# v's 1x1 convolution inside the scan of the image before, two of v's taps as diagonal matmuls, and smaller moves of work between engines

## The chip, the cores and the metric

One NeuronCore of a Trainium2 chip runs the whole program. The time is the device time of one execution in microseconds; lower is better. Before the change, three runs gave 19038.22, 19043.21 and 19052.77 us, median 19043.21 us. Engines: PE is TensorE's matmul, PEld its weight load, DVE VectorE, ACT ScalarE, POOL GpSimd, SP SyncE, which here issues nearly all DMAs.

## What is computed

Eight images of 384 channels x 64 x 64, float32, one after the other. Each passes two layers with a residual.

```python
x = x + attention(groupnorm(x))        # layer 0
x = x + selective_scan(groupnorm(x))   # layer 1

# layer 0: 1x1 convolution, then a depthwise 3x3, for each of q, k, v
q = dwconv3x3(conv1x1(x, wq), dwq)     # the same for k and v
attn = softmax(l2norm(q) @ l2norm(k).T * temperature)   # 48x48 for each of 8 heads
out  = conv1x1(attn @ v, wproj)

# layer 1: 4 directions k, state size 16, 384 channels d, 4096 positions l
dts, Bs, Cs = split(x_proj[k] @ xs[k])
dt = softplus(dt_proj[k] @ dts + bias)
h[l] = h[l-1] * exp(dt * A) + (dt * u) * B[l]     # for every (d, n)
y[l] = sum_n h[l] * C[l]
# the four directions are added, a layer norm over channels and a gelu follow
```

## The kernel before

**Layout.** 384 channels are three blocks of 128 partitions (m or j = 0, 1, 2); 4096 positions are eight chunks of 512 (c). The loop over images b calls `channel_attention` and then `selective_scan`; the last layer norm and gelu of image b ("finishing") run inside the attention of image b+1, and after the last image in `finish`.

**Attention** works on 36 pieces of 16 image rows: 12 for k, 12 for q, then 12 for v (index t = 24 to 35, by row band p, then block m). A loop over t works on several pieces at a time: `bands` and `band` do the 1x1 convolution of piece t+2 (three matmuls for 8 rows, then ACT writes them with the bias, L370 and L374); `start_sum` and `end_sum` for piece t+1 form three tap products on ACT (L419), two sums of them on POOL (L426, L432), and put the product of the centre tap into a PSUM tile `ac`; `finish_sum` for piece t adds five taps to `ac` on DVE (L457) and the POOL sum (L462). Once the softmax is known (t = 27), `fold` makes one matrix of attention and projection; `project_in` then makes a 128x512 piece of the output by three matmuls (L603), and `project_out` adds it to x on DVE (L610), takes its statistics (L611) and stores it. The last six of these 24 come after the loop, mixed with the steps of `norm_factors` for the next image. `load_ahead` loads the next image's x in pieces for its statistics (L663).

**Scan.** 32 steps for each image: 4 directions times 8 chunks (s). One step is 12 units (r = 0 to 11: block j times group g of 4 states). A unit has four scans on DVE (L962, 512 positions each). Their inputs are `da`, an exponential on ACT (L938) in a PSUM ring of three, and `db` = w times B, one POOL product of 2048 elements (L950) in a ring of three. Four transposes on PE (L983), a copy out of PSUM on ACT (`hc`, L989) and four matmuls against `cp` (L1000) turn each state tile into y. Order on each engine is that of the program text (`pin`).

Once in a step, for the next one: `project` (24 matmuls of 128 columns over r = 0 to 5, into the one bank of pool `ps_m`), `lay_out` at r = 6 (copy to `xd` on ACT, stores to DRAM, loads `cx`), `mingle_c` at r = 7 (reorders C on POOL, L872), `turn_c` at r = 8 (one transpose into the `ps_m` bank), and at r = 9 what the text calls the burst: ACT changes to Softplus, makes three `dt`, and changes back to Exp, while DVE does two `take` and four products `cp` (L889). `weigh` makes w = x times dt on POOL (L921). `fetch` broadcasts B from DRAM by DMA.

Between attention and the first scan of an image lie the last norm, `project` and `lay_out` of step 0, three `dt`, three w on DVE, the first B by DMA and `drive(0)` on DVE (L950). ACT normalises nine pieces of x there (L1063). During step 3 `look_ahead` scales the next image's wk on ACT (r = 5) and makes its bias at r = 7: nine small matmuls on PE (L272) and one operation on DVE (L277).

Of the kernel before, what the change touches and what calls it, by code (L numbers as in the profile page):

```python
# [95 lines left out]
def tile_channel_attention_then_selective_scan(ctx: ExitStack, tc: tile.TileContext, a: dict):  # L96
# [183 lines left out]
    def load_wk(b):  # L280
        wk = big.tile([P, NJ, C], F32, tag="near", name=f"wk{b}")
        nc.sync.dma_start(wk, a["wk"].rearrange("(j p) o -> p j o", p=P))
        return wk
# [15 lines left out]
    def channel_attention(b, x, stats, before):  # L299

        pin = tc.keep_in_program_order
        with ExitStack() as st:
# [6 lines left out]
            mean, rstd, wk, bias_k = stats  # L309
# [13 lines left out]

            def load_w(n):
                wts[n] = wp.tile([P, NJ, C], F32, tag="wt", bufs=2, name=f"{n}{b}")
                nc.sync.dma_start(wts[n], a[n].rearrange("(j p) o -> p j o", p=P))
# [52 lines left out]
            def bands(t):  # L379

                w, m, p = pieces[t]
                y0 = PR * p
                if w == "v":
                    if p > 0 and m == 0:
                        if ("v", p) not in pres:
                            pres["v", p] = work.tile([P, L], F32, tag="pre", name=f"pre{b}v{p}")
                        lo = max(0, PR * (p - 1) - 1)
                        rows_ = (PR + 2) * W
                        old = pres["v", p - 1][:, : NJ * rows_].rearrange("p (m l) -> p m l", l=rows_)
                        new = pres["v", p][:, : NJ * rows_].rearrange("p (m l) -> p m l", l=rows_)  # L390
                        edges.append((new[:, :, : 2 * W], old[:, :, (y0 - 1 - lo) * W : (y0 + 1 - lo) * W]))
                    if p == 0:
                        return [(t, 0, BR), (t, BR, BR), (t, PR, 1)]
                    return [(t, y0 + 1, BR), (t, y0 + 1 + BR, BR - (p == NP - 1))]
                flat = range(2 * t + (t > 0), min(2 * t + 3, 2 * KQ))
                return [(n // 2, n % NCH * BR, BR) for n in flat]

            edges = []

            def rows_of(t):  # L400

                w, m, p = pieces[t]
                if w == "v":
                    rows_ = (PR + 2) * W
                    pre = pres[w, p][:, m * rows_ : (m + 1) * rows_]
                    return pre.rearrange("p (h w) -> p h w", w=W), max(0, PR * p - 1)
                return pres[w, m].rearrange("p (h w) -> p h w", w=W), 0
# [5 lines left out]
            def product(t, tap, dy, out=None):  # L413

                pre, lo = rows_of(t)
                y0 = PR * pieces[t][2] + dy - lo
                if out is None:
                    out = work.tile([P, PR, W], F32, tag="pr", bufs=4, name=f"pr{b}_{t}_{tap}")
                pin(nc.scalar.activation(out, pre[:, y0 : y0 + PR, :], AF.Copy, scale=weight(t, tap)))  # L419
                return out  # L420

            def start_sum(t):

                up = pieces[t][2] > 0
                q, left = product(t, 1 if up else 7, -1 if up else 1), product(t, 3, 0)
                pin(nc.gpsimd.tensor_add(q[:, :, 1:], q[:, :, 1:], left[:, :, : W - 1]))  # L426
                sums[t] = q

            def end_sum(t):
# [4 lines left out]
                product(t, 4, 0, accs[t])  # L434
# [11 lines left out]
            def finish_sum(t, mid):  # L446
# [4 lines left out]
                for tap in (0, 2, 6, 8, 7 if y0 else 1):  # L451
# [145 lines left out]
            pps = {}  # L597

            def project_in(m, c, js=range(NJ)):
                if (m, c) not in pps:  # L600
                    pps[m, c] = bank(f"pp{b}{m}_{c}")
                for j in js:
# [65 lines left out]
            for t in range(-2, T):  # L668
# [10 lines left out]
                elif t == 2:  # L679
                    load_w("wv")  # L680
                elif t == KQ - 7:
                    scale_w("v")
                elif t == KQ - 5:
# [17 lines left out]
                def half(h):  # L701
# [10 lines left out]
                    if t > KQ + 2:  # L712
                        next(last, None)
                        project()
                        next(last, None)

# [33 lines left out]
                while ready:  # L750
                    project_out(*ready.pop(0))
                if t > KQ + 2:
# [27 lines left out]
    def selective_scan(b, x1, stats1, after):  # L780

        y_d = dram.tile([L, C], F32, tag="yd", bufs=2, name=f"yd{b}")
        with ExitStack() as st:
# [18 lines left out]
            with tc.tile_pool(name=f"sn{b}", bufs=1, reuse_waits="tile") as np_:  # L802
# [5 lines left out]
                for c in range(5):  # L808
                    for j in range(NJ):
# [6 lines left out]
                        else:  # L816
# [3 lines left out]
                            ))  # L820
            def view(t, k, c):
# [47 lines left out]
            def mingle_c(s):  # L869

                cy = work.tile([NG * NQ, HP, NV], F32, tag="cy", bufs=1, name=f"cy{b}_{s}")
                pin(nc.gpsimd.tensor_copy(cy, cxs[s].rearrange("r v l -> r l v")))  # L872
# [11 lines left out]
            def spread_c(s, g):  # L884

                t = work.tile([P, NQ, HP], F32, tag="cp", bufs=8, name=f"cp{b}_{s}_{g}")
                c = pcts[s][:, g * NQ : (g + 1) * NQ].rearrange("p (q o) -> p q o", o=1)
                m = quad.rearrange("p (o l) -> p o l", o=1)
                pin(nc.vector.tensor_mul(t, m.broadcast_to([P, NQ, HP]), c.broadcast_to([P, NQ, HP])))  # L889
                cps[s, g] = t  # L890
# [25 lines left out]
            def weigh(s, j):  # L916

                k, c = steps[s][:2]
                eng = nc.vector if s == 0 else nc.gpsimd
                ws[s, j] = work.tile([P, CH], F32, tag="w", bufs=3, name=f"w{b}_{s}_{j}")  # L920
# [22 lines left out]
            def drive(u):  # L943
# [7 lines left out]
                dbs[u] = t  # L951

# [33 lines left out]
            def keep(u, lb):  # L986

                t = work.tile([P, NF, P], F32, tag="hc", bufs=6, name=f"hc{b}_{u}_{lb}")
# [3 lines left out]
            def add_up(u, lb):  # L992
# [5 lines left out]
                for f in range(NF):  # L998
                    q = NF * lb + f
                    pin(nc.tensor.matmul(  # L1000
                        py[f * HP : (f + 1) * HP, lb, :], lhsT=cps[s, g][:, q, :], rhs=hc[:, f, :],
# [28 lines left out]
            def sum_of(s, j):  # L1030

                sums[s, j] = work.tile([P, NLB, P], F32, tag="ysum", bufs=3, name=f"ys{b}_{s}_{j}")
# [15 lines left out]
            for j in range(NJ):  # L1048
                step_size(0, j, step_matmul(0, j))
                weigh(0, j)  # L1050
            warm = wp.tile([P, 1], F32, name=f"warm{b}")
            for g in range(1, NG):
                fetch(0, g)
            mingle_c(0)
            turn_c(0)
            drive(0)
# [3 lines left out]
            for c in range(5, NCH):  # L1060
                for j in range(NJ):
                    s = x1[j][:, bass.ts(c, CH)]
                    pin(nc.scalar.activation(  # L1063
                        s, s, AF.Identity, bias=shift[:, j : j + 1], scale=rstd[:, j : j + 1]
                    ))

            x_next, near = None, {}

            def look_ahead(u):
# [3 lines left out]
                if u == 2 * UN:  # L1073
                    near["w"] = load_wk(b + 1)
                if u == 3 * UN + 5:
                    scale_weights(near["w"], after[1])
                if u == 3 * UN + 7:
                    near["b"] = shift_of(big, ps_m, "m", near["w"], after[0], f"{b + 1}k")

            def unit(u):  # L1080
# [24 lines left out]
                if r in (2, 6, 10) and not last:  # L1105
                    sum_of(s, r // 4)
# [9 lines left out]
                if r == 7 and nxt:  # L1116
                    mingle_c(s + 1)
                if r == 10 and nxt:
                    weigh(s + 1, 0)
                if 0 < s < S and r in (0, 2):  # L1120
# [4 lines left out]
                added(2, o - 1)  # L1125
                decay(i0 + 2)
                kept(3, o - 1)
                if r == 6 and nxt:
# [9 lines left out]
                if burst:  # L1138
# [13 lines left out]
                    for g in range(NG):  # L1152
                        spread_c(s + 1, g)
# [5 lines left out]
                    kept(2)  # L1159
                    return  # L1160
# [10 lines left out]
                if nxt and r < 6:  # L1171
                    project(s + 1, 2 * r + 1)
                scanned(3)
                decay(i0 + 5)
                kept(2)

            for u in range(U + 1):
                look_ahead(u)
                unit(u)
                if u == 0:  # L1180
                    for g in range(NG):
                        spread_c(0, g)
# [6 lines left out]
            if x_next:  # L1189
                x_next = x_next, (*after, near["w"], near["b"])  # L1190
# [57 lines left out]
    with tc.tile_pool(name="pm", bufs=1, space=PSUM) as ps:  # L1248
# [3 lines left out]
        wk = load_wk(0)  # L1252
        scale_weights(wk, st0[1])
        x = x, (*st0, wk, shift_of(big, ps, "m", wk, st0[0], "0k"))
# [55 lines left out]
```

## Time and profile before

The profiled execution took 19037.42 us; its span is 19035.6 us. The spans of stages below are from the trace of the second image unless another is named; those of the others differ by a few microseconds.

| What | Time |
|---|---|
| last scan of an image to the first of the next | 415 to 423 us |
| first scan of an image to its last | 1943 to 1952 us |
| one step, directions 0 and 2 (median) | 60.67 us |
| one step, directions 1 and 3 (median) | 60.91 and 60.87 us |
| step 0 | 64.0 to 64.7 us |
| step 3, images 0 to 6 | 64.8 to 65.6 us |
| step 3, image 7 | 60.67 us |
| one scan on DVE, recorded, and from start to start | 1.27 and 1.18 us |
| `da` on ACT (L938) | 0.70 us |
| `hc` on ACT (L989) | 0.59 us |
| `db` on POOL (L950) | 4.59 us |
| five taps of one piece (L457), from start to start each | 1.31 us |

Recorded durations of neighbouring instructions overlap, so a sum of work is made from start to start: on ACT `da` and `hc` together take 1.09 us that way, and on PE a float32 product of 128x512 is two records of 0.43 us each.

### The profile page before, as it was taken

Reading aid. Unit: us, or ns where it says so; the run is one execution under the profiler, and the core shown is the slowest. Engines: PE = TensorE matmul, PEld = TensorE weight load, DVE = VectorE, ACT = ScalarE, POOL = GpSimd, SP = SyncE. Lnnn points to the kernel's source line nnn. Section 1 sums busy time; section 2 is a strip of 40 time slices with the busy share of each in tenths; the row PEclk is TensorE's granted clock in tenths of the full one; section 3 lists DMA queues with packets and bytes.
Section 4 is the critical chain, followed back from the end, with each engine's and each line's share of the span. In section 5 each row is a group of like instructions: output and inputs, shape, how many; then the busy total and the mean of one; then the engine's idle time right before and its main releaser. Section 6 shows DMA issues by size and latency. Waiting matters only on the chain. (4 is left out here: it accounts for less than half of the span.)

```text
span 19035.6 us, 415284 instructions
## 1 busy us (share of the span) xinstructions
PE 17213.2 (90%) x166560; PEld 9804.2 (52%) x166560; DVE 18353.2 (96%) x17552; ACT 17725.0 (93%) x29821; POOL 16891.1 (89%) x7491
## 2 busy tenths in 40 slices
PE   7999989999899998999989999899998999989998
PEld 4555545555455554555545555455554555545554
DVE  8999989999899998999989999899998999989999
ACT  6999979999799997999979999799997999979998
POOL 4999959999599995999959999599995999959998
PEclk9999999999999999999999999999999999999999
DMA  1233332333323333233332333223333233322333
GB/s 58 87 100 100 103 99 86 99 100 103 102 83 100 99 104 105 83 96 100 109 99 89 94 97 107 99 90 98 96 104 100 89 100 100 98 88 88 100 99 118
DMA packets 1199753, 1842.96 MB, mean 97 GB/s; under 512 B 154400, under 2 KB 1014816, under 8 KB 1060608
## 3 DMA queue, kind: packets, MB, share of 16 engines
q1 hardware_dynamic: 1196960, 1816.28, 29.8%
q8 instruction: 1314, 21.53, 0.5%
q14 instruction: 615, 5.04, 0.1%
q10 hardware_dynamic: 864, 0.12, 0.0%
HBM read 1497.29 MB, written 318.77 MB: 95 GB/s over the span
## 5 line engine op out<-in xcount | busy, mean ns | idle before, releaser
L950 POOL TENSOR_TENSOR db<-w,B 128x2048 f32<-128x2048 f32 x3072 | 14077.5, 4588 | 47.8 <-DVE h L962 24.9
L962 DVE TENSOR_TENSOR_SCAN h<-da,ca,db 128x512 f32<-128x512 f32 x10752 | 12723.9, 1265 | 30.7 <-ACT da L938 16.8
L983 PE MATMUL pt<-ident,h 128*128 128x128 f32 x49152 | 8164.9, 291 | 1079.4 <-ACT hc L989 882.1
L938 ACT ACTIVATE da<-dt,neg_a 128x512 f32<-128x512 f32 x12288 | 8616.7, 703 | 178.4 <-DVE h L962 171.3
L989 ACT COPY hc<-pt 128x512 f32<-128x512 f32 x12288 | 7265.4, 594 | 161.7 <-PE pt L983 77.0
L983 PEld LDWEIGHTS pt<-ident,h 128*128 128x128 f32 x49152 | 5324.2, 143 | 3958.9 <-ACT hc L989 2658.4
L1000 PE MATMUL py<-hc,cp 128*32 128x128 f32 x98304 | 5221.7, 289 | 1.2 <-ACT hc L989 1.2
L1000 PEld LDWEIGHTS py<-hc,cp 128*32 128x32 f32 x98304 | 1983.3, 109 | 2164.0 <-issue 2143.9
L962 DVE TENSOR_TENSOR_SCAN h<-da,db 128x512 f32<-128x512 f32 x1536 | 1739.5, 1209 | 65.1 <-ACT da L938 43.5
L426 POOL TENSOR_TENSOR pr<-pr,pr 128x1008 f32<-128x1008 f32 x288 | 673.1, 2337 | 1187.9 <-ACT pr L419 1156.8
L847 PE MATMUL px<-x,wx 128*44 128x128 f32 x6144 | 1580.2, 346 | 79.5 <-DVE cp L889 65.6
L921 POOL TENSOR_TENSOR w<-x,dt 128x512 f32<-128x512 f32 x744 | 1063.6, 1430 | 1.4 <-ACT dt L912 1.4
L847 PEld LDWEIGHTS px<-x,wx 128*44 128x44 f32 x6144 | 505.3, 120 | 663.5 <-issue 630.7
L904 PE MATMUL pd<-xd,wdt 128*128 128x512 f32 x1536 | 725.8, 608 | 97.5 <-DVE h L962 91.6
L432 POOL TENSOR_TENSOR pr<-pr,pr 128x1008 f32<-128x1008 f32 x288 | 574.9, 1996 | 230.7 <-ACT pr L419 165.2
L603 PE MATMUL pp<-v,mT 128*128 128x512 f32 x1152 | 545.7, 622 | 100.0 <-DVE v L462 98.9
L889 DVE TENSOR_TENSOR cp<-quad,pct 128x512 f32<-128x512 f32 x1024 | 630.4, 684 | 0.0
L976 POOL COPY ca<-h 128x4 f32<-128x4 f32 x2688 | 552.7, 206 | 0.0
L904 PEld LDWEIGHTS pd<-xd,wdt 128*128 128x128 f32 x1536 | 270.9, 189 | 397.4 <-issue 177.2
L912 ACT ACTIVATE dt<-pd,dt_bias 128x512 f32<-128x512 f32 x768 | 469.5, 679 | 2.1 <-PE pd L904 1.4
L1042 DVE TENSOR_TENSOR ys<-ys,py 128x512 f32<-128x512 f32 x576 | 388.5, 674 | 38.6 <-PE py L1000 38.6
L603 PEld LDWEIGHTS pp<-v,mT 128*128 128x128 f32 x1152 | 219.2, 198 | 359.3 <-issue 232.5
(337 smaller groups left out, 11426.5 us busy)
## 6 DMA issues: line engine op xcount, KB each, us to landing
B<-bcd SPq DMA_DIRECT2D x1024, 1024.0 KB, 5.1
yd<-ys SPq DMA_DIRECT2D x384, 256.0 KB, 5.3
ys<-yd SPq DMA_DIRECT2D x768, 128.0 KB, 3.0
yd<-ys SPq DMA_DIRECT2D x768, 128.0 KB, 5.2
x<-in_x SPq DMA_DIRECT2D x48, 1024.0 KB, 8.0
x1d<-x SPq DMA_DIRECT2D x192, 256.0 KB, 3.0
ys<-yd SPq DMA_DIRECT2D x192, 256.0 KB, 2.9
fy<-yd SPq DMA_DIRECT2D x128, 384.0 KB, 4.2
```

The costliest lines, as they stand in the source:

```text
L426: pin(nc.gpsimd.tensor_add(q[:, :, 1:], q[:, :, 1:], left[:, :, : W - 1]))
L603: pin(nc.tensor.matmul(pps[m, c], lhsT=fold_of[0][:, j, bass.ts(m, P)], rhs=vs["v"][:, j, bass.ts(c, CH)], start=j == 0, stop=j == NJ - 1,))
L847: pin(nc.tensor.matmul(split(pxs[s][:XR, :])[:, part, :], lhsT=wx[:, j, k, :], rhs=view(x1[j], k, c)[:, part, :], start=i == 0, stop=i == ...
L889: pin(nc.vector.tensor_mul(t, m.broadcast_to([P, NQ, HP]), c.broadcast_to([P, NQ, HP])))
L904: pin(nc.tensor.matmul(pd, lhsT=wdt[:, k, bass.ts(j, P)], rhs=xds[s], start=True, stop=True))
L921: pin(eng.tensor_mul(split(ws[s, j]), view(x1[j], k, c), split(dts[s, j])))
L938: pin(nc.scalar.activation(t, dts[s, j], AF.Exp, scale=neg_a[:, j, steps[s][0], n : n + 1]))
L950: pin(eng.tensor_mul(t, w.broadcast_to([P, NV, CH]), bts[s, g]))
L962: pin(nc.vector.tensor_tensor_scan(h, da, db, 0.0 if start else carries[s - 1][:, j, n : n + 1], ALU.mult, ALU.add,))
L983: pin(nc.tensor.transpose(t[:, f, :], hs[u][:, bass.ts(q, HP), :].rearrange("p l v -> p (l v)"), ident))
L989: pin(nc.scalar.copy(t, pts.pop((u, lb))))
L1000: pin(nc.tensor.matmul(py[f * HP : (f + 1) * HP, lb, :], lhsT=cps[s, g][:, q, :], rhs=hc[:, f, :], start=g == lb == 0, stop=g == NG - 1 an ...
```

## The change

It has six parts.

1. While image b is scanned, v's 1x1 convolution of image b+1 is made, for b = 0 to 6. Steps 3 to 26 each make one 128x512 piece: x of image b+1 is loaded every third step (r = 2), three matmuls stand at r = 9 (end of the burst), 10 and 11 in the `ps_m` bank, ACT writes the piece with its bias at r = 0 of the next step, and a DMA stores it to `v1_d`. wv is loaded at step 0 and scaled in steps 0 to 2 at r = 8, its bias made at step 3, r = 7; wk now comes in steps 28 to 31 in the same way. In the attention of image b+1 `load_v` reads v's bands from `v1_d` by four DMAs.
2. For those images, `add_by_pe` makes the centre tap and one more tap of v's pieces by matmuls with diagonal matrices (nine, made by DVE at the start of the attention), so ACT makes no centre product and `finish_sum` adds four taps on DVE.
3. At t = 35 the first two of three matmuls of four of the last six projections are issued.
4. At an image's start the first `db` is made from four matmuls that broadcast rows of `xd` (`first_drive`), third w goes to POOL at r = 2, and the nine normalisations of x are spread over steps 0 to 2. The Softplus table is asked for earlier.
5. `cp` is one DVE product of 2048 elements in place of four of 512.
6. `mingle_c` is a copy on ACT, at the end of r = 7, in place of POOL.

Ring sizes change too (`hc` 6 to 4, `w` 3 to 2, sums of y 3 to 2), and the loads of y move from r = 2, 6, 10 to r = 6, 7, 10.

```diff
+            if v1_d:
+                diag = wp.tile([P, NJ, 3, P], F32, name=f"diag{b}")
+                for m in range(NJ):
+                    for k in range(3):
+                        pin(nc.vector.tensor_scalar_mul(
+                            diag[:, m, k, :], ident, dws["v"][:, m, 3 * k + 1 : 3 * k + 2]
+                        ))
...
+            def load_v(p):
+                pres["v", p] = t = work.tile([P, L], F32, tag="pre", name=f"pre{b}v{p}")
+                r0, r1 = max(0, PR * p - 1), min(H, PR * (p + 1) + 1)
+                nc.sync.dma_start(
...
+            def add_by_pe(t):
+                pre, lo = rows_of(t)
+                m, y0 = pieces[t][1], PR * pieces[t][2] - lo
+                tap, dy, r0, r1 = far_tap(t)
+                for s, e in ((0, r0), (r0, BR), (BR, r1), (r1, PR)):
+                    both = r0 <= s and e <= r1
+                    for d, k in ((0, 4), (dy, tap))[: 1 + both] if e > s else ():
+                        pin(nc.tensor.matmul(
+                            accs[t][:, s:e, :], lhsT=diag[:, m, k // 3, :],
+                            rhs=pre[:, y0 + d + s : y0 + d + e, :], start=d == 0, stop=d != 0 or not both,
+                        ))
...
-                product(t, 4, 0, accs[t])
+                if helped(t):
+                    add_by_pe(t)
+                else:
+                    product(t, 4, 0, accs[t])
...
-                for tap in (0, 2, 6, 8, 7 if y0 else 1):
+                for tap in (0, 2, 6, 8) + (() if helped(t) else (far_tap(t)[0],)):
...
+                    if t == T - 1:
+                        for i in range(2 * h, 2 * h + 2):
+                            project_in(i % NJ, NCH - 2 + i // NJ, range(NJ - 1))
...
+                if v1_d and 0 <= cc < T:
+                    w, m, p = pieces[cc]
+                    if w == "q" and m > 0 and p == NP - 1:
+                        load_v(m - 1)
+                    elif w == "v" and m == NJ - 1 and p + 2 < NP:
+                        load_v(p + 2)
...
+            pin(nc.scalar.activation(warm, small["dt_bias"][:, 0, 0:1], AF.Softplus))
...
-                pin(nc.gpsimd.tensor_copy(cy, cxs[s].rearrange("r v l -> r l v")))
+                pin(nc.scalar.copy(cy, cxs[s].rearrange("r v l -> r l v")))
...
+                t = work.tile([P, n, HP], F32, tag="cp", name=f"cp{b}_{s}")
...
+            def first_drive():
+                t = dbs[0] = work.tile([P, NV, CH], F32, tag="db", bufs=3, name=f"db{b}_0")
+                for v, (pool, tag) in enumerate(((ps_y, "py"), (ps_y, "py"), (ps_m, "m"), (ps_t, "t"))):
+                    pb = pool.tile([P, CH], F32, tag=tag, name=f"pb{b}_{v}")
+                    pin(nc.tensor.matmul(
+                        pb, lhsT=ident[:, R + v : R + v + 1].broadcast_to([P, P]), rhs=xds[0],
+                        start=True, stop=True,
+                    ))
+                    pin(nc.vector.tensor_mul(t[:, v, :], ws[0, 0], pb))
...
+            first_drive()
             mingle_c(0)
             turn_c(0)
-            drive(0)
             drive(1)
...
+            def v_product(s, j):
+                if next_piece(s):
+                    c, m = next_piece(s)
+                    if j == 0:
+                        near["p"] = ps_m.tile([P, CH], F32, tag="m", name=f"pv{b}_{c}_{m}")
+                    pin(nc.tensor.matmul(
+                        near["p"], lhsT=near["v"][:, j, bass.ts(m, P)], rhs=near["x"][:, j, :],
+                        start=j == 0, stop=j == NJ - 1,
+                    ))
+            def v_store(s):
+                if next_piece(s):
+                    c, m = next_piece(s)
+                    t = work.tile([P, CH], F32, tag="va", bufs=1, name=f"va{b}_{c}_{m}")
+                    pin(nc.scalar.activation(t, near["p"], AF.Identity, bias=near["bv"][:, m : m + 1]))
+                    nc.sync.dma_start(v1_d[m, :, bass.ts(c, CH)], t)
...
-                if u == 3 * UN + 5:
-                    scale_weights(near["w"], after[1])
-                if u == 3 * UN + 7:
-                    near["b"] = shift_of(big, ps_m, "m", near["w"], after[0], f"{b + 1}k")
+                for n, w, s0 in (("v", "wv", 0), ("w", "wk", 28)):
+                    j = s - s0
...
+                    if 0 <= j < NJ and r == 8:
+                        pin(nc.scalar.activation(
+                            near[n][:, j, :], near[n][:, j, :], AF.Copy, scale=rstd[:, j : j + 1]
+                        ))
+                    if j == NJ and r == 7:
+                        near["b" + n] = shift_of(big, ps_m, "m", near[n], mean, f"{b + 1}{w[1]}")
...
+                if r == 2:
+                    v_load(s)
...
+                if r == 0:
+                    v_store(s - 1)
...
+                    v_product(s, 0)
                     return
...
+                if r > 9:
+                    v_product(s, r - 9)
...
+                if raw and r in (3, 7, 11):
+                    normalise()
+                if r == 7 and nxt:
+                    mingle_c(s + 1)
```

## The prediction

> **What bounds the kernel now.** The page's first part shows four engines near full, so a mean names no bound.
>
> ```profile
> PE 17213.2 (90%) x166560; PEld 9804.2 (52%) x166560; DVE 18353.2 (96%) x17552; ACT 17725.0 (93%) x29821; POOL 16891.1 (89%) x7491
> ```
>
> I cut the trace by stage. In the scan DVE hardly pauses: 48 scans of 1.18 us from start to start, four `cp` of 0.59 and three sums of 0.58 make 60.7 us, the step of 60.67. But the timeline around the burst (start, length, engine, line) shows that ACT is level with it there:
>
> ```profile
> 1043.24 1.07 ACT L989 COPY hc<-pt 128x512 f32<-128x512 f32 x2
> 1044.33 1.28 ACT L1142 ACT_TABLE_LOAD   x1
> ...
> 1045.73 1.82 ACT L912 ACTIVATE dt<-pd,dt_bias 128x512 f32<-128x512 f32 x3
> 1047.58 1.28 ACT L938 ACT_TABLE_LOAD   x1
> 1048.87 1.30 ACT L938 ACTIVATE da<-dt,neg_a 128x512 f32<-128x512 f32 x2
> ```
> ```profile
> 1046.61 2.46 DVE L889 TENSOR_TENSOR cp<-quad,pct 128x512 f32<-128x512 f32 x4
> 1048.98 0.69 DVE L1042 TENSOR_TENSOR ys<-ys,py 128x512 f32<-128x512 f32 x1
> 1049.67 15.39 DVE L962 TENSOR_TENSOR_SCAN h<-da,ca,db 128x512 f32<-128x512 f32 x13
> ```
>
> The first `da` after the burst ends at 1049.56 and its scan starts at 1049.67; by DVE's own work it could start at 1049.56 too. PE stands idle in the burst and is then slow:
>
> ```profile
> 1050.74 0.66 PE L983 MATMUL pt<-ident,h 128*128 128x128 f32 x4 [2.28 <-ACT hc L989]
> ...
> 1052.95 1.11 PE L983 MATMUL pt<-ident,h 128*128 128x128 f32 x4
> ```
>
> Four transposes take 0.66 us, after the gap of 2.28 us some take 1.11; the granted clock from 1051.4 to 1056 is 0.63.
>
> Between the scans I read the second image's attention by stretches (us, PE, PEld, DVE, ACT, POOL, clock, DMA share, GB/s), then DVE's waits there and after:
>
> ```profile
> 2612.00:2660.00 48.00, 35.72 (x108) 18.67 (x107) 40.60 (x60) 35.24 (x53) 19.11 (x9) 0.86 0.28 89
> 2660.00:2735.00 75.00, 71.17 (x209) 33.40 (x208) 67.26 (x79) 59.54 (x93) 43.91 (x22) 1.00 0.80 265
> 2735.00:2764.00 29.00, 17.79 (x54) 8.29 (x53) 28.19 (x31) 14.80 (x22) 14.88 (x9) 0.86 0.47 161
> ```
> ```profile
> DVE x L610 <- PE pp L603: 21.4, 13, 3.9
> ```
>
> v's pieces run from 2612 to 2764. PE is the fullest engine in the middle stretch, DVE in the last; the longest wait is for projections on PE.
>
> **v in the attention (7 images).** Off DVE go 12 taps of 1.28 us from start to start, 15.3 us an image. ACT loses its convolution copies (0.69) and centre products (1.11) and isn't late there. PE loses the convolution, 32.2 us of the middle stretch by that line's own answer, and gets 4 diagonal products a piece: 8 records of 0.43 = 3.44 us, 7 pieces in the stretch, 24 us. So PE gives back 8 us where it bounds; DVE loses some 5.4 pieces x 1.28 = 7 there. They agree, and the other stretches are DVE's: 3 pieces before the softmax, 3 after: 8 us. Sum 15. Against it: `add_by_pe` needs the `ac` tile that `finish_sum` of two pieces earlier frees, and the next projections queue behind it on PE; and two of the four loads of v (3 x 128 x 18 x 64 x 4 = 1.77 MB each) fall into the middle stretch. It moves 265 GB/s at a share of 0.80, 331 at full, so they take 5.3 us each: 60 + 11 = 71 us of DMA in some 67. The loads of x for the next statistics stand behind them on SP; DVE already waits 0.2 us for one. Bounds: 0 (all lost to queueing) and 18; I take 12.8: the sum less half of the 4.5 us by which DMA exceeds its stretch, as a wait on DVE. 7 x 12.8 = **-90 us**. The nine diagonals (0.28 each) fall into DVE's idle 9.1 us before 2405, while it waits for the first loads: nothing; uncovered, 2.5 an image.
>
> **Last projections (8 images).** After v is ready at 2763.6 DVE waits for PE before each of the six sums, longest before the second:
>
> ```profile
> 2770.30 0.69 DVE L610 TENSOR_TENSOR x<-x,pp 128x512 f32<-128x512 f32 x1 [3.08 <-PE pp L603]
> ```
>
> PE then makes 6 x 3 products of 0.86 = 15.5 us and two averages for the norm; the sixth sum ends at 2785. PE was idle for 7.75 us before, so the 8 products issued early (6.9 us) are hidden there. After: four last products of 0.86 with sums of 1.33 between them, the two averages of 1.6 in between, then two full ones of 2.6; I get the sixth sum at about 2777.5, 7.3 us sooner. 8 x 7.3 = **-58 us** (bounds 4 and 8).
>
> **Start of a scan.** POOL decides it:
>
> ```profile
> 2805.89 1.76 POOL L872 COPY cy<-cx 64x128 f32<-64x128 f32 x1 [21.16 <-DMA cx<-bcd]
> 2807.78 18.06 POOL L950 TENSOR_TENSOR db<-w,B 128x2048 f32<-128x2048 f32 x4
> ```
>
> `drive(1)` is issued twice, so unit 1 waits for the second, to 2816.8. So the first `db` by PE and the normalisations moved away free DVE and ACT, not the start; and `da` now stands behind the copy of C on ACT, which waits for the same load (2805.9), then 0.3, a table load of 1.28 and 0.69: first scan at about 2808.3 for 2807.5. POOL may start up to 1.9 us sooner, but gets the third w (1.43) in step 0, where it bounds. I take +0.5 (from -2 to +2): **+4**.
>
> **Steps.** (a) One `cp` of 2048 is nearest to the 2048 product of DVE, 2.29 us, for 2.37: at most 0.2 less, in the burst, where ACT then ends last: nothing. (b) POOL loses 0.36 us. Directions 1 and 3 take 60.89, with DVE waiting for `db` at r = 4; they can fall to 60.67: 0.22 x 16 x 8 = **-28**. (c) The copy of C on ACT: between 0.20 (one element) and 0.58 (512), 0.3. Its load lands about 3 us before ACT gets there. With v's copy (0.69 recorded, 0.6 from start to start) ACT has 58.2 of 60.67 us of work, if `da` isn't late: `da` is 0.1 us ahead after the burst, gains 0.07 a scan up to 1.5, and is 1.0 to 1.2 ahead at r = 0. So 0.6 is covered. (d) v's three products, 2.6 us a step: the first lies in PE's gap of 2.28 us, the others in units without `project` (0.84 free). Nothing. The waits added for the `ps_m` bank (PE for `cp`, PE for v's copy) last tenths, before work with as much room.
>
> Here a rule speaks: the Trainium skill, "TensorE: Matmul & The Clock Gate", section "Why this matters for your kernels", lets PE drop to half its clock after idle gaps of over some 3 us. By it a gap of 2.28 us is harmless, v's products cost 2.6 us always, and the filled gap buys nothing. By the row PE is cold after it (in 7 of 10 steps a set of transposes at r = 10 is slow), so that either the filled gap cures this, or the products at r = 10 and 11 cost up to twice. I go by the row, and expect the cure: 0.86 us less of idleness. Not cured, it is the first rival.
>
> (e) The bias of the weights at step 3:
>
> ```profile
> 3030.79 0.16 DVE L277 TENSOR_SCALAR bias2k<-pb2k 128x3 f32<-128x3 f32 x1 [3.82 <-PE pb2k L272]
> ```
>
> DVE reaches it before PE has done the unit and the nine small products. Step 3 costs 4.5 us more than others in seven images. After, there are two such waits of 3.8, and six scalings of 0.6 just ahead of a burst that needs ACT's full lead, 0.4 each: 10.0 - 4.5 = 5.5, x 7 = **+38**. (f) Nine normalisations (0.70 each), three of them with the copy of C ahead of a burst: 2 us an image, **+16**. Ring sizes: `w` is freed in POOL's own order, `hc` is read one unit before reuse, the y loads keep 10 us: nothing.
>
> **Sum.** -90 - 58 + 4 - 28 + 38 + 16 = -118. The profiled execution took 19037.4: 18919. The median of the runs is 5.8 above it: **18925 us**.
>
> **Rivals.**
> - *PE cold behind the burst* (slower). The product at r = 10 costs 1.72, that at r = 11 0.86, v's copy with the bank's wait 0.9: 3.5 us in 12 scans. PE's transposes are only 0.0 to 0.4 us ahead of ACT there in cold steps, `da` 1.0 ahead, and ACT gains 0.8. DVE would wait some 1.4 us in 168 steps, +235: 19160. It decides from 118/168 = 0.7 us a step. For it: the low clock. Against it: the gap is filled. Chance 0.18.
> - *v's stretch gives nothing*, because projections behind the diagonal products, or x's loads behind v's, take DVE's place: 18925 + 90 = 19015. For it: PE 71 of 75 us, DMA at 0.80. Against it: PE's own sum falls by 8 us. Chance 0.16.
> - *The burst is not ACT's*: POOL's and DVE's savings both count, 0.17 x 248 = 42 us more: 18883. For it: ACT and DVE lie within 0.1 us. Chance 0.14.
> - That v's convolution isn't hidden at all is the first rival at full size; that the first B by TensorE does nothing is in the forecast.
>
> **How the numbers follow.** The forecast has 0.52, its own range is 18880 to 18970. Changes under 0.2% (38 us) can't be told from none. Faster: the forecast, the third rival, a third of the second: 0.71. Same: the rest of the second, 0.11. Slower: 0.18. The range, 18845 to 19085, leaves out the far end of the first rival and the lowest values of the third.
>
> **What would show it.** Right: v's pieces in about 137 us for 152, the sixth sum 7 us after v's last row sooner, two waits near 3.8 us at L277's place in each of seven images, steps 4 to 26 at 60.7 in all directions, transposes at r = 10 near 0.66. Wrong: steps 4 to 26 above 61.4, DVE waiting for `da` at r = 11 or 0, or long waits for the loads of x in the attention.

## The result, and the profile after

The changed kernel takes 19111.61 us in the median of six runs (19106.56 to 19122.27) against 19043.44 us for the kernel before beside it (19038.22 to 19052.77): 1.0039 times, with a 95% interval of 1.0027 to 1.0051. The forecast was a gain, 18925 us, and its range ended at 19085. The change made the kernel slower.

The span grew from 19035.6 to 19108.7 us, by 73.1. Cut at the first and last scan of each image:

| Stage | Before | After | Difference | Predicted |
|---|---|---|---|---|
| scans of eight images | 15584.2 | 15701.0 | +116.8 | about +26 |
| between the scans, seven times | 2937.6 | 2898.9 | -38.7 | about -138 |
| ahead of the first and behind the last scan | 513.9 | 508.9 | -5.0 | about -7 |

First the page's sum of busy time, then its group of the scans after and before (count, busy and mean time, and behind the bar's second part the idle time just before them on DVE, with what ended it).

```profile
PE 17453.1 (91%) x167254; PEld 9878.9 (52%) x167254; DVE 18215.2 (95%) x16779; ACT 17560.6 (92%) x29959; POOL 16808.9 (88%) x7243
```
```profile
L1035 DVE TENSOR_TENSOR_SCAN h<-da,ca,db 128x512 f32<-128x512 f32 x10752 | 12722.9, 1265 | 139.5 <-ACT da L1000 136.2
```
```profile
L962 DVE TENSOR_TENSOR_SCAN h<-da,ca,db 128x512 f32<-128x512 f32 x10752 | 12723.9, 1265 | 30.7 <-ACT da L938 16.8
```

DVE has 138 us less to do, as the change intends, yet the span is longer: its scans stand 119 us more before `da`. The timelines of ACT and DVE around the burst of step 11 in image 0 (direction 1) show where.

```profile
1171.34 1.28 ACT L1262 ACT_TABLE_LOAD   x1
```

```profile
1173.07 2.27 DVE L951 TENSOR_TENSOR cp<-quad,pct 128x2048 f32<-128x2048 f32 x1
1175.25 0.69 DVE L1115 TENSOR_TENSOR ys<-ys,py 128x512 f32<-128x512 f32 x1
1176.68 3.63 DVE L1035 TENSOR_TENSOR_SCAN h<-da,ca,db 128x512 f32<-128x512 f32 x3 [0.74 <-ACT da L1000]
```

Before, the first scan after the burst came 0.11 us after its `da`, with no wait to speak of. Now 0.74 us are lost there: ACT's first table load starts 1.73 us ahead of DVE's `cp`, where before it started 2.28 us ahead (1044.33 and 1046.61 in the prediction's lines). In images 0 to 6 the steps of direction 1 (10 to 14) take 61.2 us for 60.9, those of direction 3 (26 to 28) 61.1 to 61.2 for 60.9; directions 0 and 2 stand at 60.67 and 60.75 for 60.67. In image 7, which makes no v, direction 1 stands at 60.65 to 60.83.

### The profile page after: what moved, and what is told of

Its sections match the earlier page's. It is cut to its first block, busy times and chain, and to the rows that moved or that the text cites. A ratio compares the mean times of both kernels' runs of the same rounds, so it can differ in the third digit from the quotient of the medians.

```text
span 19108.7 us, 416248 instructions
## 1 busy us (share of the span) xinstructions
PE 17453.1 (91%) x167254; PEld 9878.9 (52%) x167254; DVE 18215.2 (95%) x16779; ACT 17560.6 (92%) x29959; POOL 16808.9 (88%) x7243
## 5 line engine op out<-in xcount | busy, mean ns | idle before, releaser
L1056 PE MATMUL pt<-ident,h 128*128 128x128 f32 x49152 | 8063.4, 288 | 913.0 <-ACT hc L1062 677.0
L1062 ACT COPY hc<-pt 128x512 f32<-128x512 f32 x12288 | 7342.9, 600 | 191.9 <-PE pt L1056 72.9
L1168 PE MATMUL pv<-xa,wv 128*128 128x512 f32 x1008 | 559.2, 637 | 41.7 <-DVE cp L951 36.9
L951 DVE TENSOR_TENSOR cp<-quad,pct 128x2048 f32<-128x2048 f32 x256 | 580.3, 2267 | 0.0
```

Source lines behind the costliest of these rows:

```text
L951: pin(nc.vector.tensor_mul(t, m.broadcast_to([P, n, HP]), c.broadcast_to([P, n, HP])))
L1056: pin(nc.tensor.transpose(t[:, f, :], hs[u][:, bass.ts(q, HP), :].rearrange("p l v -> p (l v)"), ident))
L1062: pin(nc.scalar.copy(t, pts.pop((u, lb))))
```

## The experiments

All times are medians, beside runs of the kernel before on the same chip; ratios are to it. Runs 1 to 4 stand beside 19035.94 us, runs 5 to 8 beside 19041.19 and runs 9 to 12 beside 19038.89, so a difference between runs of different groups, or to the changed kernel (beside 19043.44), carries up to 7.5 us besides. Steps and waits are from the one profiled execution of each run.

**1. The early projections alone.** The kernel before, with part 3 of the change and nothing else:

```diff
+                js = [j for j in js if (m, c, j) not in early]
+                early.update((m, c, j) for j in js)
...
+                    if t == T - 1:
+                        for i in range(2 * h, 2 * h + 2):
+                            project_in(i % NJ, NCH - 2 + i // NJ, range(NJ - 1))
```

> The kernel before with the third part alone: the first two products of four of the last six projections issued at t = 35. Theory: the gain of 7.4 us an image that the changed kernel shows in the tail is real and stays, so 18985 us (19043 - 59), the scan's steps and v's stretch as before. Rival: the time that the tail wins is given back at the start of the scan, where POOL waits for its B: 19040.

18971.17 us (five runs), ratio 0.9966, interval 0.9953 to 0.9979. This is 65 us under the kernel before beside it, and beats both kernels. From v's last row to the sixth sum 12.9 to 13.1 us pass in all images but the last (9.6), where they were 19.7 to 21.0 (16.3). DVE's tail in the changed kernel looks the same; the waits left are those of the two full projections:

```profile
2787.37 0.67 DVE L659 TENSOR_TENSOR x<-x,pp 128x512 f32<-128x512 f32 x1
...
2791.03 0.69 DVE L659 TENSOR_TENSOR x<-x,pp 128x512 f32<-128x512 f32 x1 [2.20 <-PE pp L652]
...
2793.61 0.69 DVE L659 TENSOR_TENSOR x<-x,pp 128x512 f32<-128x512 f32 x1 [1.16 <-PE pp L652]
```

**2. Everything but v's part.** The changed kernel, with v made in the attention again:

```diff
-            if b + 1 < B:
+            if False:
...
-                for n, w, s0 in (("v", "wv", 0), ("w", "wk", 28)):
+                for n, w, s0 in (("w", "wk", 28),):
```

> The changed kernel with v's convolution back in the attention and all five taps on DVE (parts 1 and 2 undone), the other parts kept. Theory A (v's work in the scan makes ACT late in directions 1 and 3, and v's loads disturb the attention): steps of images 0 to 6 become those of image 7 in the changed kernel, 60.7 in all directions, the scan loses some 80 us of its 117, and the time is 19025. Rival B (the copy of C on ACT makes ACT late by itself): directions 1 and 3 stay at 61.2, the time stays above 19090.

19072.57 us, 1.0019 (1.0010 to 1.0028). Theory A is half right: without v it is 39 us faster (32 when each is set against its own kernel before), yet 101 us slower than run 1. So a large part of the loss lies in parts 4 to 6 and the ring sizes. In its trace, an execution 29 us above the median, steps 26 and 27 fall to 60.66 in most images, though C is still copied by ACT. Direction 1 falls to 60.66 in images 0 and 2 and stands near 61.6 in the others, in the slower rhythm that the last section describes.

**3. x's loads ahead of v's on SP.** `load_ahead` is called before `load_v` instead of after it:

```diff
+                if t > KQ + 2:
+                    load_ahead()
                 if v1_d and 0 <= cc < T:
...
-                if t > KQ + 2:
-                    load_ahead()
```

> The changed kernel with the loads of the next image's x issued ahead of v's load in an iteration. If the wait of 9 to 11 us on that load in six images comes from standing directly behind v's load: it goes, 19058 us (54 less). If it comes from the amount of data (share 0.88 in that stretch), which makes every landing late and with it SP's queue, the wait stays, in this place or the next: above 19095.

19102.06 us, 1.0034 (1.0021 to 1.0047), and v's pieces still take 153 to 160 us. The order of these two in SP's queue isn't the cause.

**4. C reordered by POOL again**, at the place it had before:

```diff
-                pin(nc.scalar.copy(cy, cxs[s].rearrange("r v l -> r l v")))
+                pin(nc.gpsimd.tensor_copy(cy, cxs[s].rearrange("r v l -> r l v")))
```

> The changed kernel with C reordered by POOL at its old place (part 6 undone). Theory A: DVE wins back 0.3 us of ACT's lead ahead of the burst in directions 1 and 3 but POOL bounds them again near 60.9 to 61.1, 19085 us. Rival B (the copy of C is what makes ACT late): steps of directions 1 and 3 at 60.9 everywhere, as before the change, even ones at 60.67, and 19050 or less.

19072.54 us, 1.0018 (1.0009 to 1.0028): 39 us less than with the copy on ACT (32 against their own kernels before). Steps of direction 1 fall to 60.90 in the median, those of direction 3 to 60.87: what they took before the change, although v's products and copies are still there. The copy is not free on ACT, though its own record is only 0.45 us.

**5 and 6. Which part of v costs in the steps?** In run 5 ACT's copy is left out, in run 6 PE's products:

```diff
-                    pin(nc.scalar.activation(t, near["p"], AF.Identity, bias=near["bv"][:, m : m + 1]))
-                    nc.sync.dma_start(v1_d[m, :, bass.ts(c, CH)], t)
+                    nc.sync.dma_start(v1_d[m, :, bass.ts(c, CH)], near["x"][:, m, :])
```
```diff
-                        near["p"] = ps_m.tile([P, CH], F32, tag="m", name=f"pv{b}_{c}_{m}")
-                    pin(nc.tensor.matmul(
...
+                    near["p"] = near["x"][:, m, :]
```

> The changed kernel with ACT's copy of v's pieces (0.69 us, in steps 3 to 26 at r = 0) left out: the three products on PE stay, but nothing reads them, and the DMA stores a row of x in place of the piece, so v is not v. Theory A (in directions 1 and 3 it is ACT that is over-full: the copy of v and the copy of C take the lead that da needs at the burst, PE's products only fill a gap): steps 4 to 15 and 18 to 26 fall from 61.2 (direction 1) and 61.1 (direction 3) to 60.7 to 60.8, scans together about 15630 for 15701, median about 19040. Rival B (PE's products delay the transposes and the projections, and ACT waits for PE): steps stay at 61.1 or above, 19095 to 19110.

> The changed kernel with the three products of v's pieces on PE left out: ACT copies a row of x with the bias in their place, so v is not v; ACT's work is the same, only its wait of 0.28 us for PE is gone. Theory A (ACT over-full): most of the loss stays, steps of direction 1 at 61.0 to 61.2, 19075 to 19110; and transposes at r = 10 get slow again in most steps (about 7 of 10, as before the change), because PE's gap is as wide as before. Rival B (PE's products): steps of directions 1 and 3 back to 60.7 to 60.9, about 19050.

Run 5: 19127.61 us, 1.0044 (1.0027 to 1.0060). Run 6: 19111.74 us, 1.0035 (1.0022 to 1.0048). Neither gives time back. Run 5 lies above both of its theories; 6 of its 16 us lie in image 7, which makes no v and here falls into the slower rhythm. Run 6 lies 2 us above the range of its theory A, whose reason (ACT over-full) run 5 denies. Steps of direction 1 stay at 61.2 in run 5; in run 6 their median is 61.02, with single steps from 60.76 to 62.01. So either delay alone is nearly enough, and something must keep the engines from catching up afterwards. Run 6 does settle one point. In the 168 steps that make v, a set of the transposes behind the burst takes over 0.85 us in 3; with the products left out in 123, and before the change in 118. With the product in the burst's gap PE is not slow there.

What holds the engines back shows in PE's timeline of the changed kernel, in step 11 of image 0 (from its start at 1124.88):

```profile
1125.46 1.12 PE L1168 MATMUL pv<-xa,wv 128*128 128x512 f32 x2
1126.42 0.60 PE L1056 MATMUL pt<-ident,h 128*128 128x128 f32 x4
...
1130.68 0.61 PE L908 MATMUL px<-x,wx 128*44 128x128 f32 x2
1131.22 0.66 PE L1056 MATMUL pt<-ident,h 128*128 128x128 f32 x4
1131.80 0.43 PE L1073 MATMUL py<-hc,cp 128*32 128x128 f32 x8
1132.16 0.66 PE L1056 MATMUL pt<-ident,h 128*128 128x128 f32 x4
1132.75 0.42 PE L1073 MATMUL py<-hc,cp 128*32 128x128 f32 x8
1133.10 0.61 PE L908 MATMUL px<-x,wx 128*44 128x128 f32 x2
```

There is no gap in these lines. A set of `project` (`px`), two sets of transposes and two of `py` come round every 2.42 us (1130.68 to 1133.10), a unit of twice that every 4.84 us; DVE's four scans take 4.71 (1.177 from start to start). PE loses 0.13 a unit, an estimated 0.8 us from r = 0 to r = 5. In directions 0 and 2 a `px` takes 0.41 us for 0.61, since x is read in contiguous columns. Before the change PE entered these units with room enough to lose that. Now v's product of r = 11 stands in r = 0 (1125.46), or ACT's copy holds up the `hc` that PE waits for: either uses up the room.

**7. Half of v's load in the attention.** The third and fourth band aren't loaded:

```diff
+                if p > 1:
+                    pres["v", p] = pres["v", 1]
+                    return
```

> The changed kernel with the third and fourth band of v not loaded: pieces 24 to 35 read the second band a second time (v of the lower half of the image is that of another band), so 3.5 MB an image less pass over DMA and over SP's queue, just where the loads of x for the next statistics wait. Theory A (the 10.9 us wait of DVE for x in images 1 to 6 comes from the amount of data in the middle stretch): the wait goes, v's twelve pieces take 143 to 149 us for 155, and the time falls by 6 x 8 = some 50 us, to about 19060. Rival B (the pieces are bound by PE, where diagonal products and projections queue): v's pieces stay at 153 to 158, and the time at 19100 or above.

19084.12 us, 1.0023 (1.0014 to 1.0033): 27 us less, half of what theory A said. The time between scans falls by 32.5 us in sum (2898.9 to 2866.4), v's pieces take 149 to 155 us. DVE's waits in v's stretch of image 1 (sum, times, longest), of the changed kernel and of this one:

```profile
DVE x L659 <- PE pp L652: 12.1, 6, 7.1
DVE st L712 <- DMA qT<-in_x: 11.3, 2, 10.9
DVE v L509 <- PE pa L540: 4.2, 1, 4.2
```
```profile
DVE x L662 <- PE pp L655: 12.0, 6, 7.0
DVE v L512 <- PE pa L543: 7.6, 1, 7.6
DVE st L715 <- DMA gm<-in_x: 5.6, 2, 3.7
```

The wait for x falls from 11.3 to 5.6, and PE's wait ahead of the first piece takes back 3.4 of it. Over seven images the waits for x in v's stretch sum to 64.6 us in the changed kernel, 30.9 here and 7.8 before the change; the stretch itself is 34 us shorter here than in the changed kernel.

**8. No v, and C by POOL**: the edits of runs 2 and 4 together.

> The changed kernel without v's part (the convolution in the scan and the diagonal taps), and with C reordered by POOL as before: the early projections, the changed start, the one product for C's weights and the ring sizes are left. Theory A (C's copy on ACT is what costs in steps without v too, the rest nearly nothing): about 18990 to 19030, steps of direction 1 at 60.7 to 60.9, close to the kernel with the early projections alone (18971). Rival B (the changed start, the merged product or the smaller rings cost): 19060 or above, 16 and 24 and the first three steps as slow as in the changed kernel.

19031.42 us, 0.9995 (0.9986 to 1.0005). Without v too, C on ACT costs about 40 us (19072.57 less 19031.42; 46 against their own kernels before). So v and C on ACT each cost some 30 to 50 us of the whole, with the other or without it; what is left of parts 4 and 5 and the rings still costs 60 us against run 1 (55 against their own kernels before). The profiled execution, 29 us above the median, is 100 us longer than that of run 1. In it steps 0 to 2 take 36 us more than in run 1 in images 0 to 6, step 31 16 more, step 3 29 less, steps 7 to 14 and 23 to 30 23 more, image 7 8 more, and between the scans 38 us are lost: after v's last row 16 to 19 us pass in three images for 12.9. Which ring or product does that wasn't taken apart.

**9. `project` always in direction 0's order.** B, C and step sizes of directions 1 and 3 are then taken at wrong places; the work is otherwise that of the changed kernel.

```diff
-                    rhs=view(x1[j], k, c)[:, part, :], start=i == 0, stop=i == PX * NJ - 1,
+                    rhs=view(x1[j], 0, c)[:, part, :], start=i == 0, stop=i == PX * NJ - 1,
```

> The changed kernel with one thing altered: the six matmuls of `project` in each step read x always in the order of direction 0 (contiguous columns), so B, C and the step sizes of directions 1 and 3 are taken at wrong places. In the trace a set of these for one half takes 0.41 us in contiguous order and 0.61 us in the order of directions 1 and 3; with them PE's unit at r = 1 to 5 is about 4.86 us against the 4.71 of DVE's four scans. Theory A (in directions 1 and 3 PE, behind by v's product or ACT's copy at r = 0, can't catch up before r = 6, ACT waits for PE, and the burst begins without da's full lead): steps 4 to 14 of direction 1 and 3 fall from 61.2 and 61.1 to 60.7 to 60.8, scans together about 15630 to 15650 for 15701, median about 19050. Rival B (these steps are slow for another reason, for example the DMA traffic of v or ACT's own work): steps stay at 61.0 or above, 19095 to 19115.

19011.45 us (ten runs): 100 us less than the changed kernel, 40 more than theory A had. Steps 10 to 14 take 60.65 to 60.67 us (one 61.02), with v's products and copies as they were. PE's timeline at the same place of the step:

```profile
1122.67 0.42 PE L908 MATMUL px<-x,wx 128*44 128x128 f32 x2
1123.02 0.66 PE L1056 MATMUL pt<-ident,h 128*128 128x128 f32 x4
1123.60 0.43 PE L1073 MATMUL py<-hc,cp 128*32 128x128 f32 x8
1123.96 0.66 PE L1056 MATMUL pt<-ident,h 128*128 128x128 f32 x4
1124.55 0.43 PE L1073 MATMUL py<-hc,cp 128*32 128x128 f32 x8
1124.90 0.42 PE L908 MATMUL px<-x,wx 128*44 128x128 f32 x2
```

2.23 us for a round, 4.46 for a unit: PE gains on DVE. And DVE's waits in the whole of step 11, of the changed kernel and of this one:

```profile
DVE h L1035 <- ACT da L1000: 0.7, 1, 0.7
```
```profile
DVE h L1035 <- ACT da L1000: 0.2, 1, 0.2
```

The lead of `da` (from its end to the start of its scan, medians over steps 10 to 14 of images 0 to 6, from the instructions' times) ties this together:

| Kernel | scan 0 | scan 3 | scan 16 | scan 38 | step |
|---|---|---|---|---|---|
| before | 1.01 | 1.22 | 1.66 | 2.11 | 60.9 |
| changed | 1.19 | 0.51 | 0.83 | 1.50 | 61.2 |
| without ACT's copy | 1.18 | 1.40 | 0.82 | 1.48 | 61.2 |
| without PE's products | 0.95 | 0.55 | 1.03 | 1.69 | 61.0 |
| `px` contiguous | 1.18 | 0.51 | 1.43 | 2.11 | 60.7 |
| C by POOL, with v (run 4) | 1.19 | 0.51 | 1.02 | 2.05 | 60.9 |

The burst begins at scan 38. ACT needs the full 2.11 there to be done with its table loads in time: 0.61 short is 0.5 longer a step. With `px` contiguous v's copy takes its 0.9 at scan 3 as in the changed kernel, but ACT, no longer held by PE, regains it. The last row shows that v alone leaves nearly all of the lead: the step's 60.9 is then what POOL allowed before the change. In direction 3 without v but with C on ACT (run 2) the lead at scan 38 is 2.11 too. The shortfall in these steps takes both.

**10. Normalisations ahead of the scan again.**

```diff
+            while raw:
+                normalise()
```

> The changed kernel with the nine normalisations of x put back ahead of the scan's first step instead of steps 0 to 2. Theory A (they cost 0.7 us each in the steps, since ACT can't regain the lead before the burst, and nothing ahead of the scan, where POOL sets the start): steps 0, 1 and 2 fall from 66.3, 62.8 and 62.2 by 1 to 2 us each, the start stays at 24 us, together -25 to -40 us, about 19078. Rival B (they cost as much ahead of the scan, as ACT's copy of C and the first da stand behind them): the start grows by 4 to 6 us, the sum is 0 or up, 19105 to 19125.

19112.39 us, 1.0038 (1.0023 to 1.0052): no change. Steps 0 to 2 fall by 12 us in images 0 to 6, steps 7 to 9 grow by 5, the start stays at 24, and image 7 takes 7 us more in the slower rhythm. Spreading them costs about what was foreseen in the steps and doesn't explain the loss.

**11. Early projections, and the first B by TensorE** (`first_drive` in place of `drive(0)`).

> The kernel before with the early projections (measured 18971) and, of part 4, the first B by TensorE alone; the normalisations, the third w on DVE and C on POOL stay as before. Theory A (POOL sets the start, and loses one product of 4.6 us, so unit 1 starts sooner): first step and start together 2 to 4 us an image less, about 18945 to 18955. Rival B (DVE's four products and the second product on POOL stand in the same place, nothing gained): 18965 to 18980, or worse by DVE's 2.6 us an image, 18990.

18971.28 us, 0.9962 (0.9947 to 0.9977): the same as run 1, so rival B. The first scan comes about 2 us sooner and the first step is 2.1 us longer. POOL's timeline says why, here and in run 1:

```profile
437.35 0.39 POOL L877 COPY cy<-cx 64x128 f32<-64x128 f32 x1 [21.52 <-DMA cx<-bcd]
439.47 13.52 POOL L955 TENSOR_TENSOR db<-w,B 128x2048 f32<-128x2048 f32 x3 [1.72 <-DMA B<-bcd]
```
```profile
437.14 1.39 POOL L877 COPY cy<-cx 64x128 f32<-64x128 f32 x1 [21.47 <-DMA cx<-bcd]
439.26 13.53 POOL L955 TENSOR_TENSOR db<-w,B 128x2048 f32<-128x2048 f32 x3 [0.73 <-DMA B<-bcd]
```

POOL's product waits for the load of B, so the second unit can't start sooner whoever makes the first. In both runs the second unit's first scan starts 0.03 us after the end of the second of these products, so the double issue of `drive(1)` holds it too.

**12. The same, and the bias in step 3 written by ACT.**

```diff
+        if by_act:
+            pin(nc.scalar.activation(bias, pb[:, :NJ], AF.Copy, scale=-1.0))
```

> As the run before it, and the bias of the next image's k weights in step 3 is written by ACT instead of DVE. Theory A (step 3 is slow only because DVE, a unit ahead of PE, stands 3.8 us before PE's nine small products; ACT runs just behind PE and waits less than 1 us): step 3 falls from 65.1 to 61.5 or below, 7 x 3.5 = 25 us less than the run before it, about 18925. Rival B (the scalings on ACT and PE's lag make step 3 slow): step 3 stays above 64, no gain.

18974.48 us, 0.9966 (0.9952 to 0.9979); step 3 stays at 65.0 us. Theory A falls: the wait moves to `da`, which now stands behind the bias on ACT.

```profile
3018.66 2.07 PE L272 MATMUL pb2k<-mean,wk 128*128 128x1 f32 x18
3020.76 0.17 ACT L278 ACTIVATE bias2k<-pb2k 128x3 f32<-128x3 f32 x1 [2.60 <-PE pb2k L272]
...
3021.55 3.63 DVE L981 TENSOR_TENSOR_SCAN h<-da,ca,db 128x512 f32<-128x512 f32 x3 [2.44 <-ACT da L946]
```

What is left is PE's 2.07 us for products of one column, at a place where all three engines follow each other closely. In the changed kernel, where the scalings lie in other steps, step 3 with such a bias is still 2.9 us longer than 60.67, for a wait of 2.75. So the bias explains the larger part of the 4.3 us here; what the scalings on ACT (rival B) add wasn't taken apart.

## Why the prediction was wrong, point by point

- **The steps, (b), (c) and (d): the first step that failed.** The prediction let `da` gain 0.07 us a scan up to its cap, and so held v's copy and products, with C's copy, covered by the lead. In directions 0 and 2 that holds. In directions 1 and 3 the gain ends where PE's unit with `px` (4.84 us) is longer than DVE's (4.71): ACT can't run ahead of the PE it copies for. The row was in the profile before; the prediction took PE's spare time of 0.84 from units without `project`, and put nothing beside those with it. For steps 7 to 14 and 23 to 30 of images 0 to 6 some 25 us less were foreseen, as POOL's relief; they took 60 more. Run 9 shows the cause: with `px` contiguous they fall by 92. Part of these 92 isn't the change's: the kernel before has the same long sets, and its steps lie 32 us above those of run 9. What it would gain wasn't measured.
- **C on ACT (c), put at nothing:** 39 us of the whole, by run 4; 30 of them by the traces in the steps just named. It takes 0.25 of lead at scan 34, four scans ahead of the burst, where nothing can regain it; its load in time says nothing of that. Alone it costs these steps nothing where they keep the faster rhythm (run 2: 60.66); on top of v's delay it does. So v's work alone isn't to blame for directions 1 and 3.
- **v in the attention, -90: the second step that failed, and as large.** v's stretch became 4 us longer in sum over seven images. What came in place of the taps, in image 1: 11.1 us more of waiting for x, 2.7 for the first piece's PE, 1.9 for projections, against the 15 us of taps. DVE's waits there before the change:

```profile
DVE x L610 <- PE pp L603: 10.2, 7, 3.9
DVE v L462 <- PE pa L493: 1.5, 1, 1.5
DVE st L663 <- DMA qT<-in_x: 0.2, 1, 0.2
```

  The wait for x makes up 57 of the 94 us by which this term missed (64.6 for 7.8 in seven images). Image 7, which loads no next x, has none, and its stretch is 5 us shorter than before (146.7 for 152.0). The second rival gave this stretch nothing, and that came. The prediction had named the projections and x's loads; it priced DMA's excess at 4.5 us and half of it as a wait. These are the windows (us, then PE, PEld, DVE, ACT, POOL, clock, DMA share, GB/s) and the wait:

```profile
2628.00:2680.00 52.00, 38.25 (x108) 19.79 (x109) 36.61 (x57) 31.04 (x47) 23.36 (x11) 0.84 0.55 183
2680.00:2745.00 65.00, 51.02 (x148) 24.95 (x147) 50.72 (x61) 35.52 (x56) 32.07 (x17) 0.87 0.88 294
2745.00:2782.00 37.00, 34.82 (x108) 16.89 (x107) 33.15 (x39) 19.85 (x31) 23.03 (x14) 1.00 0.48 164
```
```profile
2728.49 1.29 DVE L712 BATCH_NORM_STATS2 st<-qT 128x6 f32<-128x512 f32 x2 [10.90 <-DMA qT<-in_x]
```

  In the middle DMA carries 294 GB/s for 265 and PE and DVE both pause. SP's timeline (start, length, queue, line) and its waits from 2700 to 2725 show where x's load was late.

```profile
2701.99 0.43 SPq L704 DMA_DIRECT2D gm<-in_x  x1
...
2707.33 0.44 SPq L414 DMA_DIRECT2D pre1v<-v1d  x1
...
2722.14 0.81 SPq L704 DMA_DIRECT2D qT<-in_x  x1
```
```profile
SPq L214 <- DMA out<-fy: 10.5, 3, 4.5
```

  20 us lie between two loads of x that before came 2 to 11 apart, and SP stands 10.5 us at loads of the finish whose tile a store has yet to free. It stood there as long before (13.6 us from 2685 to 2710), so this view gives the place of the delay, not its cause. Run 3 excludes the mere order of v's and x's loads. Run 7 shows that v's third and fourth loads cause about half of the wait; whether by their data or by their place in SP's queue it doesn't tell apart.
- **Last projections, -58:** right. 7.3 us an image, eight times, 58; alone it brought 65 us of measured time (run 1).
- **Start, +4:** right in size (+4.7 in sum), and the first B by TensorE does nothing, as said (run 11), because POOL starts when B has landed and the second unit waits for POOL's second product, the double issue that the prediction names.
- **POOL relief, -28:** right where it can be seen: in image 7 direction 1 fell from 60.9 to mostly 60.67. In the others it drowned.
- **Bias and scalings, +38:** too high. Step 3 fell by 1.6 us, step 31 rose by 2.3: 5 us in seven images, and some tenths for scalings. The wait was 2.8 and 2.1 us instead of 3.8, and PE's clock stayed at 1.00 behind the first.
- **Normalisations, +16:** right in the steps (12 us in seven images), and no gain elsewhere (run 10).
- **PE cold behind the burst, the rival that ended slower:** right in sign only. The gap was filled and PE was slow behind it in 3 of 168 steps for 118 (run 6). By the Trainium skill, "TensorE: Matmul & The Clock Gate", section "Why this matters for your kernels", only gaps of over some 3 us matter; here one of 2.28 us did, and the row was the better guide. But PE's lateness came back by another way, at r = 0.

Not settled: why parts 4 and 5 and the ring sizes cost some 55 to 60 us without v and without C on ACT (run 8), and with it the larger part of steps 0 to 2, which took 38 us more in images 0 to 6 (12 of them the normalisations). The kernel before with `px` contiguous wasn't run. Not tried: reading x in `project` by rows of 8 columns in directions 1 and 3, with the transposed place written in PSUM, which would leave the result as it is.

## What to carry to other kernels

Work put "into a gap" costs nothing only if every engine downstream can regain the delay before the next point that needs its full lead. So divide the loop where the rate changes, and put each engine's round beside that of the bound one: here 4.84 against 4.71 us in six of twelve units decided what v and C cost in the steps. When several small delays each use up the same reserve, taking one away may show nothing; widen the reserve as well. And a part of a change that is simple and alone on its path may be all that is worth keeping.

## What the runs showed of the hardware

- The same 44-row products over x take 0.41 us (a pair of records) in contiguous columns and 0.61 us with a stride of 64 elements.
- After products of one column, busy by the records throughout, PE's clock was low in two traces. In run 12 it was 0.80 in the 8.5 us before them, 1.00 while they ran, then 0.55 (same columns as above):

```profile
3018.50:3021.00 2.50, 2.50 (x24) 2.48 (x24) 0.61 (x1) 0.24 (x2) 0.43 (x2) 1.00 0.41 107
3021.00:3024.00 3.00, 2.63 (x25) 1.36 (x23) 2.45 (x3) 3.00 (x6) 3.00 (x2) 0.55 0.64 265
```

  Transposes then take 1.12 us for 0.66. After the same products of v's bias in the changed kernel the clock stayed at 1.00, so it doesn't always happen, and that these products are the cause isn't shown.
- The scan settles in one of two rhythms. In image 7, where the changed kernel and that of run 7 do the same work, steps 4 to 6 take 60.66 to 60.67 us in the first's trace and 61.43 to 61.47 in the second's; at step 6 `da`'s lead at scan 0 is 0.68 there and 0.09 here. The kernel before has the slower one as well: 61.44 to 61.45 in steps 4 to 6 of image 1, where most other images have 60.66. What tips it wasn't looked for.
